# Edge keys computed behind the casts of the first weight chunk, and two row loads asked for behind chunk 4

## The chip, the core and the metric

The kernel runs on one core of a Trainium2 chip. The metric is the device time of one execution in microseconds (us). Before the change three runs gave 299.84, 299.84 and 300.05 us, so the median is 299.84.

The engines named below are TensorE (PE, with its weight loads shown as PEld), VectorE (DVE), ScalarE (ACT), GpSimd (POOL) and SyncE (SP), whose only work here is to issue transfers. Each engine runs its instructions in the order in which they were written, and waits for the others by semaphores.

## The reference, cut to what matters

One graph layer on 384 nodes with 1024 features and 16 heads of 64:

```python
h = relu(layernorm(x))
q, k, v = h @ wq.T + bq, h @ wk.T + bk, h @ wv.T + bv
q2, k2, v2 = (q @ wiq.T + biq), (k @ wik.T + bik), (v @ wiv.T + biv)   # split into 16 heads
mask = full((384, 384), -inf)
mask[src, dst] = softplus(edge_type_weights)[edge_type - 1]            # 6528 edges; of a repeated edge the last one counts
mask[i, i] = softplus(edge_type_weights)[3] where it is still -inf
out = softmax(q2 @ k2.T / 8 + mask) @ v2
return x + (out @ wo.T + bo)
```

Edges repeat, and the last of a set of equal (src, dst) pairs decides the cell. That is why the kernel compares edge keys.

## The kernel before, in words

**The dense path.** x comes in three tiles of 128 nodes. For each tile VectorE takes the statistics (`ln_bn`, `ln_mean`, L247 and L250), the mean is subtracted (`ln_sub`: ACT and POOL share tiles 0 and 1, VectorE does tile 2), TensorE transposes the tile (`ln_transpose`, L288), and the relu and the split into a high and a low part follow (`ln_hi`, L295 and L297; `ln_lo`, L302). A product in the working precision is made of three matmuls (high by high, high by low, low by high: L368 to L370). The division by the standard deviation is done later, on the products (`rrow`).

**Weights.** They are streamed in 56 chunks of 128 x 1024 (512 KB), named by a running number `w`. `load(w)` (L65) asks for one on SP's queue into one of four buffers, so that chunk w waits for the low part of chunk w - 4. `split_hi` casts a chunk to its high part (L77, on ACT), `split_lo` subtracts (L82, on VectorE or POOL). Chunk 0 is cast in two halves on VectorE (L344) and subtracted on POOL (L346). Chunks 0 and 1 go through `pieces` (L380), which orders their products by what is ready first: chunk 0 by tiles 0 and 1 (256 columns), then by tile 2, then its low part, and so on. From chunk 2 on one chunk is 24 matmuls.

**The edges.** The 6528 edges lie in 51 columns of 128; the columns are divided among three tables in DRAM of 384 x 384 cells. A key is src * 384 + dst. It is needed in two layouts: by columns on the partitions (`mask_floats`, `mask_keys` on POOL) and as rows. For the rows, `key_rows` computes 128 x 51 keys on VectorE from `er` (L180), and stores them to the DRAM tensor `krow` on SP's queue (L181). `key_load(g, s)` (L201) reads six columns of table s back, broadcast to all 128 partitions (384 KB); group 0 is loaded in the prologue, groups 1 and 2 during the projections. `mask_detect` (L213, VectorE) compares a column's keys with the row and counts later duplicates; `mask_index` (L219, L220) makes an index of it that sends overridden edges to a dump cell; `mask_scatter` (L224, POOL) writes the values to the tables, which `table_clear` (L145, SP) has cleared. The first three comparisons are written behind chunk 1's slot, one for each table. Their index shares a tile with the edge values that POOL computes (L171 to L174). Later the tables are read back and put over the mask.

**What sets the order.** The order in each engine's queue is the order of the calls in the text (`manual_schedule`); the prologue is written out by hand, and so are the slots of the projections (`slot_head`, then the products, then the edge work of the slot, `detect`). On SP's queue the prologue stands in this order: x (three tiles), `er`, chunk 0, `ed`, chunk 1, the biases, the edge type weights, the store of the keys, chunks 2 and 3, three row loads, chunk 4, then chunk 5 and the clears.

Of the kernel before, what the change touches and what calls it, by code (L numbers as in the profile page):

```python
# [14 lines left out]
N, D, NT, KT, NP = 384, 1024, 3, 8, 8  # L15
# [7 lines left out]
def gnn_kernel(ctx: ExitStack, tc: tile.TileContext, x, edges, erows, etw, wq, wk, wv, wiq, wik, wiv, wo,  # L23
# [6 lines left out]
    nc = tc.nc  # L30
# [9 lines left out]
    NTAB, RNG = 3, EC // 3  # L40
# [19 lines left out]
    def load(w):  # L60
        if w >= NCH:
            return
        n, m = chunks[w]
        raw[w] = wpool.tile([128, D], F32, tag="raw", name="raw", bufs=4)
        nc.sync.dma_start(raw[w], W[n][m])  # L65
# [112 lines left out]
    def key_rows():  # L178

        nc.vector.scalar_tensor_tensor(krt[:, :EC], er[:, :EC], float(N), er[:, EC:], op0=OP.mult, op1=OP.add)  # L180
        nc.sync.dma_start(krow.rearrange("c j -> (c j)").rearrange("(p e) -> p e", p=128), krt[:, :EC])  # L181
# [5 lines left out]
    def parts(g):  # L187
        return [(r * RNG + g * PA, min(r * RNG + (g + 1) * PA, (r + 1) * RNG)) for r in range(NTAB)]
# [3 lines left out]
    def key_load(g, s):  # L192

        if s == 0:
            t = work.tile([128, 2, NT, N], F32R, tag="pt", name="rows")
            krv[g] = t.bitcast(F32).rearrange("p a k n -> p (a k n)")
        c0, c1 = parts(g)[s]
        dst = krv[g][:, s * PA * 128:(s * PA + c1 - c0) * 128]
        for c in range(c0, c1):
            rows[c] = krv[g][:, (s * PA + c - c0) * 128:(s * PA + c - c0 + 1) * 128]  # L200
        nc.sync.dma_start(dst, krow[c0:c1, :].rearrange("c j -> (c j)").partition_broadcast(128))  # L201
# [47 lines left out]
    def ln_mean(t):  # L249
        nc.vector.bn_aggr(lnt[:, 2 * t:2 * t + 2],  # L250
                          lnt[:, 30 + 12 * t:42 + 12 * t].rearrange("p (a b) -> p a b", a=2))
        if t < 2:
            nc.scalar.mul(negm[:, t:t + 1], lnt[:, 2 * t:2 * t + 1], -1.0)
# [19 lines left out]
    def ln_sub(t, c0, c1, eng):  # L273
        src, dst = xt[t][:, c0:c1], xn[t][:, c0:c1]
        if eng is nc.scalar:
            nc.scalar.activation(dst, src, AF.Identity, bias=negm[:, t:t + 1])
        elif eng is nc.gpsimd:
            nc.gpsimd.tensor_tensor(dst, src, lnt[:, 2 * t:2 * t + 1].to_broadcast([128, c1 - c0]), OP.subtract)
        else:
            nc.vector.tensor_scalar(dst, src, lnt[:, 2 * t:2 * t + 1], None, op0=OP.subtract)  # L280

    def ln_transpose(t):
        pss = []
        for half in range(2):
            ps = bank("st"[half] if t < 2 else "ga"[half])
            for j in range(4):
                k = half * 4 + j
                nc.tensor.transpose(ps[:, j * 128:(j + 1) * 128], xn[t][:, k * 128:(k + 1) * 128], ident)  # L288
            pss.append(ps)
        return pss  # L290

    def ln_hi(t, half, ps, eng=None):
        hi = hT[:, 0, half * 4:half * 4 + 4, t * 128:(t + 1) * 128]
        if eng is None:
            nc.scalar.activation(hi, ps.rearrange("p (k n) -> p k n", k=4), AF.Relu)  # L295
        else:
            eng.tensor_scalar(hi, ps.rearrange("p (k n) -> p k n", k=4), 0.0, None, op0=OP.max)  # L297
# [28 lines left out]
    ln_bn(2, 0)  # L326
    ln_bn(2, 1)
    ln_mean(2)
    key_rows()
    load(2)  # L330
    load(3)
    for s in range(NTAB):
        key_load(0, s)
    ln_sub(2, 0, 512, nc.vector)
    ln_sub(2, 512, D, nc.vector)
    p1 = ln_transpose(1)
    warm(WARM[2])
    ln_hi(1, 0, p1[0])
# [3 lines left out]
    whl[0] = (t0[:, 0, :], t0[:, 1, :])  # L342
    for c in (slice(0, 512), slice(512, D)):
        nc.vector.tensor_copy(t0[:, 0, c], raw[0][:, c])  # L344
    for c in (slice(0, 512), slice(512, D)):
        nc.gpsimd.tensor_tensor(t0[:, 1, c], raw[0][:, c], t0[:, 0, c].bitcast(F32), OP.subtract)  # L346
    load(4)
    ln_hi(2, 0, p2[0], nc.vector)
    ln_hi(2, 1, p2[1])
    split_hi(1)  # L350
# [535 lines left out]
```

## Time and profile before

| | |
|---|---|
| median of three runs | 299.84 us |
| the profiled execution | 298.95 us |
| its span (first to last instruction) | 297.2 us |
| TensorE busy | 291.2 us, 98% of the span |
| VectorE, POOL, ACT busy | 202.4, 155.7, 153.8 us |
| share of TensorE in the chain that ended last | 96% |
| DMA, mean over the span | 185 GB/s |
| TensorE clock granted | full in every slice |

The profile page divides the span into 40 slices of 7.4 us and gives each engine's busy tenths in each. The chain that ended last is followed back from the last instruction, at each step to what released it. A timeline line has the start in us from the span's start, the time taken, the engine, the line of the kernel, the operation, what it writes and reads, how many were merged, and in brackets the idle time before it with what ended it. SPq lines are transfers that SP issues; their time is that of the issue, not of the transfer. TensorE's matmuls overlap, so that the durations of single ones add up to more than the time they take.

### The profile page before, as it was taken

The page shows a single profiled execution, that of the slowest core. Times are in us where ns is not written, and L with a number is a line of the kernel's source. Part 1 is how long each engine was busy: PE and PEld are TensorE (multiplying, and loading weights), DVE is VectorE, ACT ScalarE, POOL GpSimd, SP SyncE. Part 2 cuts the span into 40 slices and gives each one's busy share as a digit, 9 for nine tenths or more (in the row PEclk, how much of TensorE's full clock was granted, in tenths as well). Part 3 has the DMA queues.
Part 4 walks back from the last instruction along what each step waited for, and adds up shares of the span by engine and source line. Part 5 has one row for each costly group of instructions (what it writes and reads, how often), then busy time and mean ns, then how long its engine had stood idle before and what let it go on. Part 6 is the DMA issues. An engine that isn't in the chain of part 4 may idle for free.

```text
span 297.2 us, 4982 instructions
## 1 busy us (share of the span) xinstructions
PE 291.2 (98%) x1654; PEld 276.5 (93%) x1654; DVE 202.4 (68%) x495; ACT 153.8 (52%) x288; POOL 155.7 (52%) x160
## 2 busy tenths in 40 slices
PE   6999999999999999999999999999999999999995
PEld 5999999999988889999999999999999998888884
DVE  4958977766856553888865676868686766696423
ACT  3784644433422222554336677778777767865310
POOL 3774567363857785710033656373746467976210
PEclk9999999999999999999999999999999999999999
DMA  7899864645396648393369784738374656900005
GB/s 279 277 324 398 292 207 131 225 143 212 116 303 202 197 153 289 113 342 112 117 167 261 206 216 115 202 93 223 99 221 121 170 144 176 348 10 0 2 3 209
DMA packets 22377, 55.12 MB, mean 185 GB/s; under 512 B 4816, under 2 KB 8400, under 8 KB 22352
## 3 DMA queue, kind: packets, MB, share of 16 engines
q1 hardware_dynamic: 19968, 52.42, 56.0%
q0 software_dynamic: 2064, 1.80, 2.1%
q10 hardware_dynamic: 320, 0.59, 0.9%
q8 instruction: 13, 0.21, 0.3%
q14 instruction: 12, 0.10, 0.1%
HBM read 40.39 MB, written 4.97 MB: 153 GB/s over the span
## 4 chain that ended last, share of the span: by engine, by line
PE 96%; DVE 1%; DMA 1%; ACT 0%; issue 0%
PE g L370 21%; PE g L368 21%; PE g L369 21%; PE a L758 6%; PE s L721 6%; PE t L741 5%; PE g L380 3%; PE s L369 2%; PE s L370 2%; PE s L368 2%; PE t L370 2%; PE t L369 2%; PE t L368 2%; DMA g<-in_x_dram 1%; DVE lnt L247 1%; PE a L369 1%
## 5 line engine op out<-in xcount | busy, mean ns | idle before, releaser
L368 PE MATMUL g<-g,whl 128*128 128x384 f32 x304 | 103.6, 341 | 0.0
L370 PE MATMUL g<-g,whl 128*128 128x384 f32 x304 | 101.8, 335 | 0.0
L369 PE MATMUL g<-g,whl 128*128 128x384 f32 x304 | 101.5, 334 | 0.0
L224 POOL DMA_INDIRECT tab<-val,idx x51 | 56.1, 1100 | 37.5 <-issue 11.0
L77 ACT ACTIVATE whl<-raw 128x1024 fp32r<-128x1024 f32 x51 | 53.6, 1051 | 29.7 <-PE g L370 21.1
L82 DVE TENSOR_TENSOR whl<-raw,whl 128x1024 fp32r<-128x1024 f32 x41 | 52.6, 1282 | 15.6 <-ACT whl L77 12.4
L736 POOL TENSOR_TENSOR e<-e,s 128x384 f32<-128x384 f32 x48 | 39.3, 829 | 43.1 <-DVE s L735 42.4
L369 PEld LDWEIGHTS g<-g,whl 128*128 128x128 f32 x304 | 57.2, 188 | 0.0
L368 PEld LDWEIGHTS g<-g,whl 128*128 128x128 f32 x304 | 57.1, 188 | 0.0
L370 PEld LDWEIGHTS g<-g,whl 128*128 128x128 f32 x304 | 57.0, 188 | 0.0
L82 POOL TENSOR_TENSOR whl<-raw,whl 128x1024 fp32r<-128x1024 f32 x11 | 26.4, 2398 | 30.8 <-ACT whl L77 28.1
L390 ACT ACTIVATE g<-f,bc 128x384 fp32r<-128x384 f32 x24 | 14.8, 618 | 52.7 <-DVE f L389 41.2
L751 DVE TENSOR_TENSOR pt<-t,pt 128x384 fp32r<-128x384 f32 x48 | 26.4, 549 | 15.3 <-ACT pt L750 15.0
L731 ACT ACTIVATE e<-e,s 128x384 f32<-128x384 f32 x48 | 29.2, 608 | 9.3 <-DVE s L727 8.1
L750 ACT ACTIVATE pt<-t 128x384 fp32r<-128x384 f32 x48 | 23.3, 486 | 13.6 <-PE t L741 13.3
L727 DVE CUSTOM_DVE_ANT_0 e<-s,ma 128x384 f32<-128x384 f32 x48 | 26.4, 549 | 3.6 <-PE s L721 3.4
L721 PE MATMUL s<-ks,qs 128*128 128x384 f32 x96 | 24.7, 338 | 0.0
L741 PE MATMUL t<-ident,e 128*128 128x128 f32 x144 | 23.5, 271 | 0.0
L389 DVE TENSOR_TENSOR f<-g,rrow 128x384 f32<-128x384 f32 x24 | 13.3, 556 | 13.9 <-PE g L370 13.7
L741 PEld LDWEIGHTS t<-ident,e 128*128 128x128 f32 x144 | 18.7, 140 | 3.1
L758 PE MATMUL a<-pt,vhl 128*128 128x384 f32 x96 | 20.8, 351 | 0.0
L721 PEld LDWEIGHTS s<-ks,qs 128*128 128x128 f32 x96 | 17.5, 188 | 0.8
(145 smaller groups left out, 416.2 us busy)
## 6 DMA issues: line engine op xcount, KB each, us to landing
ks<-nat SPq DMA_DIRECT2D x30, 192.0 KB
raw<-in_wv_dram SPq DMA_DIRECT2D x8, 512.0 KB
raw<-in_wq_dram SPq DMA_DIRECT2D x8, 512.0 KB
raw<-in_wiv_dram SPq DMA_DIRECT2D x8, 512.0 KB
raw<-in_wk_dram SPq DMA_DIRECT2D x8, 512.0 KB
raw<-in_wiq_dram SPq DMA_DIRECT2D x8, 512.0 KB
raw<-in_wik_dram SPq DMA_DIRECT2D x8, 512.0 KB
raw<-in_wo_dram SPq DMA_DIRECT2D x8, 512.0 KB
```

Of the source, the lines that this page charges most:

```text
L77: nc.scalar.activation(dst[0], raw[w], AF.Copy)
L82: (eng or nc.vector).tensor_tensor(lo, raw[w], hi.bitcast(F32), OP.subtract)
L224: nc.gpsimd.indirect_dma_start(out=tabs[c // RNG], out_offset=bass.IndirectOffsetOnAxis(ap=idx[:, c:c + 1], axis=0), in_=val[:, c:c + 1], ...
L368: nc.tensor.matmul(ps, lhi, rhi, start=first, stop=False)
L369: nc.tensor.matmul(ps, lhi, rlo, start=False, stop=False)
L370: nc.tensor.matmul(ps, llo, rhi, start=False, stop=last)
L721: nc.tensor.matmul(ps[:, :N], qs[:, o, t * 128:(t + 1) * 128], ks[:, o, s, :], start=(s == 0), stop=(s == 1))
L727: nc.vector.tensor_tensor_reduce(e, st_ps.pop(i)[:, :N], ma[:, t, :], -0.125, 3.0e38, OP.add, OP.min, s[:, 0:1])
L731: nc.scalar.activation(es[i], es[i], AF.Exp, bias=s[:, 0:1], scale=-1.0, accum_out=s[:, 1:2])
L736: nc.gpsimd.tensor_tensor(es[i], es[i], s[:, 2:3].to_broadcast([128, N]), OP.mult)
L741: nc.tensor.transpose(ps[:, k * 128:(k + 1) * 128], es[i][:, k * 128:(k + 1) * 128], ident)
L758: nc.tensor.matmul(ps[:, :N], vhl[:, k, p, 2 * o:2 * o + 2, :], pts[h][:, s, k, :], start=(k == 0 and s == 0), stop=(k == 2 and s == 1))
```

## The change

`key_rows()` (one VectorE instruction and the store that SP issues) goes from just behind the statistics of tile 2 to just behind the two casts of chunk 0 on VectorE. The subtraction of tile 2's mean and the loads of chunks 2 and 3 so come ahead of it. Of the three row loads of group 0, the one for table 0 follows the store, and those for tables 1 and 2 are asked for behind chunk 4. Nothing is added and nothing removed.

```diff
@@ -326,13 +326,10 @@
     ln_bn(2, 0)
     ln_bn(2, 1)
     ln_mean(2)
-    key_rows()
+    ln_sub(2, 0, 512, nc.vector)
+    ln_sub(2, 512, D, nc.vector)
     load(2)
     load(3)
-    for s in range(NTAB):
-        key_load(0, s)
-    ln_sub(2, 0, 512, nc.vector)
-    ln_sub(2, 512, D, nc.vector)
     p1 = ln_transpose(1)
     warm(WARM[2])
     ln_hi(1, 0, p1[0])
@@ -342,9 +339,13 @@
     whl[0] = (t0[:, 0, :], t0[:, 1, :])
     for c in (slice(0, 512), slice(512, D)):
         nc.vector.tensor_copy(t0[:, 0, c], raw[0][:, c])
+    key_rows()
+    key_load(0, 0)
     for c in (slice(0, 512), slice(512, D)):
         nc.gpsimd.tensor_tensor(t0[:, 1, c], raw[0][:, c], t0[:, 0, c].bitcast(F32), OP.subtract)
     load(4)
+    key_load(0, 1)
+    key_load(0, 2)
     ln_hi(2, 0, p2[0], nc.vector)
     ln_hi(2, 1, p2[1])
     split_hi(1)
```

## The prediction

> **What bounds the kernel now.** I read the page first (engine shares, the 40 slices, the chain that ended last), then the chain in order of time for the first 20 us, then the timeline of that stretch engine by engine, with SP's queue, and last the busy times by stretches of 1 us with the DMA rate.
>
> ```profile
> PE 291.2 (98%) x1654; PEld 276.5 (93%) x1654; DVE 202.4 (68%) x495; ACT 153.8 (52%) x288; POOL 155.7 (52%) x160
> PE   6999999999999999999999999999999999999995
> PE 96%; DVE 1%; DMA 1%; ACT 0%; issue 0%
> ```
>
> TensorE is the bound: full in every slice but the first and the last, and 96% of the chain. So a change counts only if it moves TensorE's first real matmul, or opens a gap later. The chain of the first 20 us shows the first:
>
> ```profile
> 8.23 0.66 PE s L288 x4
> 8.89 0.45 PE t L288 x4
> 9.34 0.63 PE g L288 x4
> 9.97 0.44 PE a L288 x4
> 10.41 8.16 PE g L380 x52
> ```
>
> From 8.23 on TensorE follows itself: transposes of tiles 1 and 2, then the products of w0 and w1, then everything else. The timeline shows what feeds them, and the other ends of the change:
>
> ```profile
> 8.46 0.21 DVE L250 BATCH_NORM_AGGREGATE lnt<-lnt 128x2 f32<-128x12 f32 x1
> 8.59 0.16 DVE L180 SCALAR_TENSOR_TENSOR kr<-er 128x51 f32<-128x51 int32 x1
> 8.71 0.88 DVE L280 TENSOR_SCALAR g<-g,lnt 128x512 f32<-128x512 f32 x2
> 8.78 0.33 SPq L181 DMA_DIRECT2D krow<-kr  x1
> 9.15 0.91 SPq L65 DMA_DIRECT2D raw<-in_wv_dram  x2
> 9.31 0.42 PEld L288 LDWEIGHTS g<-ident,g 128*128 128x128 f32 x4 [0.22 <-issue]
> 9.51 0.76 DVE L344 CAST whl<-raw 128x512 fp32r<-128x512 f32 x2
> 10.01 2.66 POOL L346 TENSOR_TENSOR whl<-raw,whl 128x512 fp32r<-128x512 f32 x2 [1.70 <-DVE whl L344]
> 10.69 1.29 SPq L201 DMA_DIRECT2D rows<-krow  x3
> 12.70 2.70 SPq L65 DMA_DIRECT2D raw<-in_wv_dram  x2
> 13.85 1.06 ACT L77 ACTIVATE whl<-raw 128x1024 fp32r<-128x1024 f32 x1 [1.49 <-DMA raw<-in_wv_dram]
> 23.34 1.06 ACT L77 ACTIVATE whl<-raw 128x1024 fp32r<-128x1024 f32 x1 [0.56 <-DMA raw<-in_wv_dram]
> 23.80 0.17 DVE L219 SCALAR_TENSOR_TENSOR ed<-cnt,key 128x3 f32<-128x3 f32 x1 [0.83 <-POOL val L174]
> ```
>
> The reader is to see: VectorE goes from the statistics of tile 2 (L250) through the key (L180) to the subtraction (L280) that tile 2's transposes at 9.31 wait for; SP issues nothing between 5.42 (4.96 + 0.46, the issue before) and 8.78, and its waits put 3.1 us there on the key of L180; two casts on ACT wait for weights (chunk 2 until 13.85, chunk 4 until 23.34).
>
> **The change part by part.**
>
> *The key leaves the place ahead of L280.* L280 starts 0.12 after L180 (8.71 - 8.59), so the most to be had is 0.12 us. But L280 reads the mean that L250 ends at 8.67 (8.46 + 0.21). In pairs where the second reads the first's result, the second starts 0.04 after the first's end: L219 23.80 + 0.17 to L220 at 24.01; L166 17.97 + 0.16 to L167 at 18.17. 8.67 + 0.04 = 8.71: where L280 stands today. L180, which does not read the mean, sits in that bubble (it starts 0.08 before L250 ends). Bounds: gain 0.00 to 0.12. I take 0.00, by the two dependent pairs, which are the same situation.
>
> The Trainium skill (VectorE: DVE Perf Modes, "The DRAIN you can't avoid" and the rules for authors) says that chained operations pay for emptying the pipe and that their count is what to lower; by that, one operation fewer ahead of L280 would be worth all of its 0.16. The trace agrees only in part, since L180 overlaps L250.
>
> *The key comes in behind the casts of w0* (now 9.51 to 10.27). It adds 0.12 (its start-to-start) ahead of ln_hi(2,0), L297, now 10.18 + 0.69 = 10.87, then 10.99. Behind L297 are the six low parts of h (L302), the root's follow-up and softplus_a, all 0.12 later until VectorE's idle time after 16.84. Who waits: TensorE's second pass of w0 (tile 2) comes after eight 256-column products, which the groups by shape give 1.2 us of busy time, 293 ns each; the last overlaps the next one's start, so the pass starts no sooner than 10.16 + 1.2 - 0.29 = 11.07. 10.99 leaves 0.08: cost 0, bound 0.1. The low parts end at 13.77 + 0.68 = 14.45, then 14.57; the last half is first used 16 matmuls of 0.173 ahead of 18.57, at 15.8: hidden by 1.2 us. POOL's L346 starts on the first cast, which lies ahead of the key and stays at 9.51: 0.
>
> *Chunks 2 and 3 no longer stand behind the key on SP.* Their two issues (0.91 together) go from 9.15 to just behind 5.42, at the latest behind the landing of x's last tile (VectorE starts on it at 7.14). The DMA rate by stretches is 378 GB/s in 6 to 8, 419 in 8 to 9, 116 in 9 to 10, 66 in 10 to 11: the queue runs dry there today, and these 2 x 512 KB fill the hole. From 10 on, 1.05 MB at 378 GB/s take 2.8 us: they land at about 12.8, chunk 2 at about 11.4. ACT's cast of chunk 2 can then start where ACT falls idle, at 13.85 - 1.49 = 12.36. What is late next: the softplus table (1.28) is loaded by 14.7, and L160 waits for softplus_a, 15.55 + 0.15 + 0.12 = 15.82, against 16.22 now. So 0.4 us earlier for ACT, POOL's values (L174) and the cast and low part of chunk 3. TensorE meets chunk 3 at 23.61, with the low part now ready at 20.44 + 1.22 = 21.66: the gain is only more slack, 0 on the sum.
>
> *The key's store.* L180 at about 10.18 releases the store on SP 0.19 later (8.59 to 8.78), 10.4; it queues behind chunks 2 and 3 and lands at about 13.3 instead of 10.69 (I allow half a us behind them). Then on SP: rows of table 0 (0.43), chunk 4 (0.33), rows 1 and 2 (0.86), from 13.3 to 14.9. Chunk 4 is issued at 13.8 instead of 12.70; chunk 5 waits for POOL until 15.06 anyway; the clears of the tables follow as now. So the queue behind the waiting SP loses nothing but chunk 4's 1.1 us, and chunk 4 gains the two row loads that it no longer stands behind.
>
> *When do the third table's rows land?* VectorE reads them at 22.59. Behind the issue at 13.3 lie at most 1.9 us (store issued to its release, 8.78 to 10.69), so data flow from 15.2 at the latest; 3 x 384 KB + 512 KB = 1.70 MB. Rates of rows: 194 and 226 GB/s in 16 to 18, where they have the queue, 324 and 347 in 18 to 20, mixed with weights. At 194 they end at 24.0, at 226 at 22.7, at 324 at 20.4. I take 22.5, between the last two, since a third of the bytes are weights.
>
> The Trainium skill (DMA: Bandwidth & Descriptors, "Specifications") has packets of 512 B and more at line rate; the rows' 3 KB packets would then end by 20. In the trace 16 to 18 contradicts it; the sum is the same by both.
>
> At 22.5 the third comparison ends at about 23.0, still before 23.80, where L219 waits for POOL's values (perhaps 23.4 with the 0.4 above). What it would cost with that cover gone: from L219 VectorE is busy through to the low part of chunk 5, 29.36 + 1.22 = 30.58. Chunk 2 starts on TensorE at 19.45 and chunk 3 at 23.61, so a chunk is 4.16 and chunk 5 starts at 31.93; weights load 0.18 ahead. Slack 1.17. L219 may slip to 24.97, so the rows may land until 24.5 before TensorE waits. Cost 0, with nothing to gain where TensorE has no gap; upper bound +0.5 (landing at 25, 1.0 beyond the slowest rate).
>
> **The sum.** 0.00 (L280; bound -0.12) + 0.00 (second pass; bound +0.10) + 0 (all DMA; bound +0.5). Against the profiled execution: 298.95 us (span 297.2 and 1.75 around it) stays 298.95, which stands 0.89 below the median of 299.84. Predicted median: 299.8.
>
> **The rivals.**
> 1. *The key's 0.12 does come off the start:* L280 at 8.59, tile 2's transposes and the casts 0.12 earlier, TensorE with them; ACT's last cast ahead of w0 (L295, 9.52 + 0.61 = 10.13) does not stop it, being needed only from the fifth matmul on. 299.84 - 0.12 = 299.72. For it: TensorE waits 0.22 before 9.31. Against: the dependent pairs.
> 2. *Slower, by the late third table:* its rows land after 24.5, VectorE stands in line behind the comparison, the low part of chunk 5 comes late. Landing at 26 costs 1.5: 301.3; just past the point, 300.0. For it: three row loads begin 2.6 us later than now, and a rows stretch at 194 GB/s ends at 24.0, 0.5 short of the point. Against: the slack, and chunks 2 and 3 already out of the queue.
> 3. *Really faster:* ACT's two waits for weights (1.49 and 0.56) were paid for by TensorE; then up to 2.0 less, 297.8. Against it: PE shows no idle time between 8.23 and the end, and every chunk's low part is ready 1.2 us or more ahead. Only small gaps below what the views print could hide it, so a fraction at best: 299.2.
>
> **How the numbers follow.** Main case (nothing on TensorE's path, 299.7 to 299.95) 0.70; rival 1 0.10; rival 2 0.12; rival 3 0.05; 0.03 is left for a shift of clock or code that no view announces, taken as within 0.2%. 0.2%, 0.6 us, is about what a measurement of this kernel can tell from no change. Main case, rival 1 and the remainder lie within it: 0.83, and rival 2 just past its point too, so of its 0.12 0.02 go there: same 0.85, slower 0.10, faster 0.05. The range goes from 299.3 (a fraction of rival 3) to 300.5 (the rows half a us past their point, 299.84 + 0.5, rounded up).
>
> **What would show it.** Right: L280 starts again 0.25 after L250, w0's first L380 again at 10.1 to 10.2; L180 behind the casts; SP's two chunk issues between 5.4 and 7.5; the store landed at 13 to 13.7; ACT's wait of 1.49 gone; L219 again held by POOL's values; PE without a gap. Wrong: L280 at 8.6 (rival 1); VectorE idle before L213 with the rows as releaser, L219 after 25, TensorE idle near 32 (rival 2); chunks starting on TensorE at less than 4.16 apart (rival 3).

## The result and the profile after

The changed kernel takes 300.72 us (median of 20 runs, 299.86 to 301.07) against 299.86 for the kernel before (20 runs beside it, 299.18 to 300.33). The ratio is 1.0024, 95% interval 1.0016 to 1.0032: slower by 0.5 to 1.0 us. The forecast was no change (299.8, range 299.3 to 300.5), so it was wrong: the loss is clear of noise, and the time lies above the range. The profiled execution of the change took 300.95 us with a span of 299.2.

From the page of the changed kernel: busy time of each engine, TensorE in 40 slices, and the chain that ended last.

```profile
PE 291.1 (97%) x1654; PEld 276.4 (92%) x1654; DVE 203.0 (68%) x495; ACT 153.8 (51%) x288; POOL 155.0 (52%) x160
PE   6799999999999999999999999999999999999995
PE 94%; DMA 2%; DVE 2%; SPq 0%; issue 0%
```

TensorE does the same work (291.1 us against 291.2) in a span 2.0 longer; the loss stands at the start, where the second slice is no longer full (7 instead of 9), and VectorE and the transfers have 2% of the chain each instead of 1%. The chain of the changed kernel in order of time shows the place (start, duration, what):

```profile
9.72 0.88 DVE g L280 x2
10.60 0.67 DVE whl L341 x2
11.27 1.22 DVE kr L180
12.50 0.61 DVE g L297
...
13.15 6.89 PE g L381 x41
```

The key, L180, is a link of 1.22 us between the casts of chunk 0 and the relu of tile 2 (L297), and TensorE's products wait for that relu. The timeline of the changed kernel, engine by engine:

```profile
8.15 1.29 DVE L247 BATCH_NORM_STATS2 lnt<-g 128x6 f32<-128x512 f32 x2 [1.10 <-DMA g<-in_x_dram]
9.47 0.21 DVE L250 BATCH_NORM_AGGREGATE lnt<-lnt 128x2 f32<-128x12 f32 x1
9.72 0.88 DVE L280 TENSOR_SCALAR g<-g,lnt 128x512 f32<-128x512 f32 x2
11.02 2.65 POOL L345 TENSOR_TENSOR whl<-raw,whl 128x512 fp32r<-128x512 f32 x2 [2.84 <-DVE whl L341]
11.15 1.01 PEld L381 LDWEIGHTS g<-g,whl 128*128 128x128 f32 x8
11.19 1.31 DVE L180 SCALAR_TENSOR_TENSOR kr<-er 128x51 f32<-128x51 int32 x1
13.15 1.11 PE L381 MATMUL g<-g,whl 128*128 128x128 f32 x8 [0.78 <-DVE g L297]
21.27 0.19 PEld L369 LDWEIGHTS g<-g,whl 128*128 128x128 f32 x1
25.30 0.17 DVE L219 SCALAR_TENSOR_TENSOR ed<-cnt,key 128x3 f32<-128x3 f32 x1 [0.83 <-POOL val L174]
```

The same instruction on 128 x 51 that took 0.16 us takes 1.31 here. It comes 0.17 after POOL's subtraction L345 has started, and TensorE waits 0.78 before its second pass of chunk 0.

Two distances sort the 2.0 us. From TensorE's first weight load of chunk 0 to that of chunk 2 (L368 before, L369 after) pass 9.13 us before (10.14 to 19.27) and 10.12 after (11.15 to 21.27): 0.99 lost there. From chunk 2 to the end of the span it is 277.9 in both (297.2 - 19.27 and 299.2 - 21.27): nothing that happens later matters. The other 1.01 us lies ahead of the first product, 10.14 against 11.15, where VectorE starts on x's third tile at 8.15, after a wait of 1.10 for it, instead of 7.14 without a wait. Whether that belongs to the change had to be found out.

### The profile page after: what moved, and what is told of

The parts are those of the page before. It is cut to its first block, busy times and chain, and to the rows that moved or that the text cites. A ratio compares the mean times of both kernels' runs of the same rounds, so it can differ in the third digit from the quotient of the medians.

```text
span 299.2 us, 4982 instructions
## 1 busy us (share of the span) xinstructions
PE 291.1 (97%) x1654; PEld 276.4 (92%) x1654; DVE 203.0 (68%) x495; ACT 153.8 (51%) x288; POOL 155.0 (52%) x160
## 4 chain that ended last, share of the span: by engine, by line
PE 94%; DMA 2%; DVE 2%; SPq 0%; issue 0%
PE g L369 21%; PE g L371 21%; PE g L370 21%; PE a L759 6%; PE s L722 6%; PE t L742 5%; PE g L381 3%; DMA g<-in_x_dram 2%; PE s L370 2%; PE s L371 2%; PE s L369 2%; PE t L371 2%; PE t L370 2%; PE t L369 2%; PE a L371 1%; PE a L370 1%
## 5 line engine op out<-in xcount | busy, mean ns | idle before, releaser
L369 PE MATMUL g<-g,whl 128*128 128x384 f32 x304 | 103.6, 341 | 0.0
L82 DVE TENSOR_TENSOR whl<-raw,whl 128x1024 fp32r<-128x1024 f32 x41 | 52.4, 1277 | 15.3 <-ACT whl L77 15.3
L369 PEld LDWEIGHTS g<-g,whl 128*128 128x128 f32 x304 | 57.1, 188 | 0.0
L82 POOL TENSOR_TENSOR whl<-raw,whl 128x1024 fp32r<-128x1024 f32 x11 | 26.4, 2399 | 30.4 <-ACT whl L77 27.7
L751 ACT ACTIVATE pt<-t 128x384 fp32r<-128x384 f32 x48 | 23.3, 486 | 13.6 <-PE t L742 13.3
L390 DVE TENSOR_TENSOR f<-g,rrow 128x384 f32<-128x384 f32 x24 | 13.3, 555 | 14.2 <-PE g L371 14.2
```

Of the source, the lines that this page charges most:

```text
L82: (eng or nc.vector).tensor_tensor(lo, raw[w], hi.bitcast(F32), OP.subtract)
L369: nc.tensor.matmul(ps, lhi, rhi, start=first, stop=False)
```

## The experiments

Theory A: the key, behind the casts, stands still beside POOL's subtraction of chunk 0 and holds up the relu of tile 2. Theory B: the early loads of chunks 2 and 3 make x's third tile land late. Theory C: the late rows of the tables. What the kernels gave (d is the time from the first weight load of chunk 0 to that of chunk 2, in the traced execution; the ratio is against the kernel before, timed on the same chip):

| run | key or added instruction, us | d, us | ratio, 95% interval |
|---|---|---|---|
| kernel before | 0.16 | 9.13 | |
| the change | 1.31 | 10.12 | 1.0024 (1.0016 to 1.0032) |
| key at its old place, SP as changed | 0.16 | 9.11 | 0.9999 (0.9989 to 1.0009) |
| key ahead of the casts | 0.20 | 9.21 | 0.9999 (0.9988 to 1.0011) |
| before, with a second key behind the casts | 1.31 | 10.12 | 1.0026 (1.0014 to 1.0039) |
| key through PSUM | 0.20 and 0.21 | 9.29 | 0.9995 (0.9983 to 1.0006) |
| POOL's subtraction in one piece | 0.21 | 9.90 | 1.0015 (1.0006 to 1.0025) |
| in four pieces | 0.21; again 0.75 | 9.07; again 9.56 | 1.0018 (1.0008 to 1.0028) |
| before, with a one-input copy behind the casts | 1.28 | 10.02 | 1.0017 (1.0006 to 1.0028) |
| 768 and 256 columns | 0.21 | 9.19 | 1.0010 (0.9996 to 1.0024) |
| before, 23 warm-up transposes | 0.16 | 9.11 | 0.9991 (0.9980 to 1.0002) |

### The two halves of the change apart

The key back at its old place, every transfer as in the change:

```diff
     ln_mean(2)
+    nc.vector.scalar_tensor_tensor(krt[:, :EC], er[:, :EC], float(N), er[:, EC:], op0=OP.mult, op1=OP.add)
     ln_sub(2, 0, 512, nc.vector)
...
     def key_rows():
-        nc.vector.scalar_tensor_tensor(krt[:, :EC], er[:, :EC], float(N), er[:, EC:], op0=OP.mult, op1=OP.add)
         nc.sync.dma_start(krow...
```

> The key's VectorE instruction goes back between the statistics and the subtraction of tile 2; SP's order stays that of the change (chunks 2 and 3 ahead of the store, rows 1 and 2 behind chunk 4). Theory A (the key behind the casts stands still beside POOL's subtraction of chunk 0 and holds up the relu of tile 2, so TensorE's second pass of chunk 0): the key takes 0.16 us again, no gap of TensorE between the first and the second pass, time that of the kernel before within 0.15 us. Theory B (the early loads of chunks 2 and 3 make x's third tile land 1.0 us later, 8.1 instead of 7.1, and with it everything): time 0.7 to 1.0 us above the kernel before. Theory C (the late rows): also 0.7 to 1.0 above, with VectorE waiting for rows.

And the other way round: the kernel before, every transfer in its place, with one more instruction of the key's form:

```diff
         nc.vector.tensor_copy(t0[:, 0, c], raw[0][:, c])
+    scrap = ert[:, 2 * EC:3 * EC]
+    nc.vector.scalar_tensor_tensor(scrap, er[:, :EC], float(N), er[:, EC:], op0=OP.mult, op1=OP.add)
     for c in (slice(0, 512), slice(512, D)):
```

> The kernel before with one more instruction of the key's form (two SBUF inputs, 128 x 51) behind the casts of chunk 0, written to unused columns; no transfer is moved. Theory A: the added instruction takes 1.2 to 1.4 us instead of 0.16, the relu of tile 2 starts 1.2 later, TensorE waits 0.8 to 1.1 before the second pass, time 0.7 to 1.0 us above the kernel before. Theories B and C: 0.16 us for the added instruction and no change of the time beyond 0.15.

The timelines, first of the key at its old place:

```profile
7.82 1.29 DVE L246 BATCH_NORM_STATS2 lnt<-g 128x6 f32<-128x512 f32 x2 [0.85 <-DMA g<-in_x_dram]
9.27 0.16 DVE L328 SCALAR_TENSOR_TENSOR kr<-er 128x51 f32<-128x51 int32 x1
10.82 8.08 PEld L381 LDWEIGHTS g<-g,whl 128*128 128x128 f32 x52
19.93 0.19 PEld L369 LDWEIGHTS g<-g,whl 128*128 128x128 f32 x1
```

then of the kernel before with the second key (L346 is the added one, L348 POOL's subtraction):

```profile
8.12 1.29 DVE L247 BATCH_NORM_STATS2 lnt<-g 128x6 f32<-128x512 f32 x2 [1.00 <-DMA g<-in_x_dram]
9.56 0.16 DVE L180 SCALAR_TENSOR_TENSOR kr<-er 128x51 f32<-128x51 int32 x1
10.98 2.64 POOL L348 TENSOR_TENSOR whl<-raw,whl 128x512 fp32r<-128x512 f32 x2 [2.74 <-DVE whl L344]
11.15 1.31 DVE L346 SCALAR_TENSOR_TENSOR er<-er 128x51 f32<-128x51 int32 x1
11.11 1.02 PEld L382 LDWEIGHTS g<-g,whl 128*128 128x128 f32 x8
13.11 7.09 PEld L382 LDWEIGHTS g<-g,whl 128*128 128x128 f32 x44 [0.98 <-DVE g L297]
21.23 0.19 PEld L370 LDWEIGHTS g<-g,whl 128*128 128x128 f32 x1
```

All of SP's part gives 0.9999; one instruction behind the casts, alone, gives 1.0026 and the d of the change to the hundredth. The same operation takes 0.16 at 9.56 and 1.31 at 11.15 in one execution, so neither its form nor its size is the cost, but the place. B and C fall. x's third tile was late in the second of these (8.12) with SP's queue exactly as before.

### The key ahead of the casts

```diff
     ln_sub(2, 512, D, nc.vector)
+    nc.vector.scalar_tensor_tensor(krt[:, :EC], er[:, :EC], float(N), er[:, EC:], op0=OP.mult, op1=OP.add)
     load(2)
```

(and gone from `key_rows`, which keeps the store.)

> The change, but the key's instruction stands between the subtraction of tile 2 and the casts of chunk 0, where POOL is idle. Theory A: the key takes 0.16 us; the casts start 0.12 later; no gap of TensorE between the passes; 0 to 0.15 us above the kernel before. Theories B and C: 0.7 to 1.0 us above.

It took 0.20 us, and 0.9999 is the time of before. Moving the key out of the wait for the mean was worth nothing, and what it cost ahead of the casts is too little to be seen (d is 0.08 longer in the one trace; the interval reaches about 0.35 us either way).

### Which instructions wait

SBUF and PSUM are the two on-chip memories that the kernel uses: most tiles lie in SBUF, the results of TensorE in PSUM. The key of the change, made by two instructions of which neither reads two SBUF tensors:

```diff
-        nc.vector.scalar_tensor_tensor(krt[:, :EC], er[:, :EC], float(N), er[:, EC:], op0=OP.mult, op1=OP.add)
+        kps = bank("g")
+        nc.vector.tensor_scalar(kps[:, :EC], er[:, :EC], float(N), None, op0=OP.mult)
+        nc.vector.scalar_tensor_tensor(krt[:, :EC], kps[:, :EC], 1.0, er[:, EC:], op0=OP.mult, op1=OP.add)
```

> The change, but the key is made behind the casts by two instructions with one SBUF input each: the product of src goes to PSUM, then PSUM times 1 plus dst. If it is two SBUF inputs that make the instruction wait for POOL (theory A, narrow form): both take 0.1 to 0.25 us, TensorE's wait before the second pass is at most 0.2, time 0 to 0.25 us above the kernel before. If any VectorE instruction on SBUF at that place waits (theory A, wide form): 1.2 us again, 0.7 to 1.0 above. Theories B and C: 0.7 to 1.0 above.

A copy with one input, added to the kernel before:

```diff
         nc.vector.tensor_copy(t0[:, 0, c], raw[0][:, c])
+    nc.vector.tensor_copy(ert[:, 2 * EC:3 * EC], krt[:, :EC])
     for c in (slice(0, 512), slice(512, D)):
```

> The kernel before with one float copy of 128 x 51 from SBUF to SBUF (one input) added behind the casts of chunk 0. If only two SBUF inputs make VectorE wait for POOL: the copy takes 0.1 to 0.2 us, no wait of TensorE, the time of the kernel before within 0.15 us. If one input of a fast SBUF copy is enough: 1.2 to 1.4 us, TensorE waits 0.8 to 1.1, time 0.7 to 1.0 us above.

The timeline of the key through PSUM:

```profile
10.28 2.66 POOL L347 TENSOR_TENSOR whl<-raw,whl 128x512 fp32r<-128x512 f32 x2 [2.00 <-DVE whl L343]
10.45 0.20 DVE L181 TENSOR_SCALAR g<-er 128x51 f32<-128x51 int32 x1
10.69 0.21 DVE L182 SCALAR_TENSOR_TENSOR kr<-g,er 128x51 f32<-128x51 f32 x1
10.41 8.26 PEld L383 LDWEIGHTS g<-g,whl 128*128 128x128 f32 x52
```

and of the one-input copy (L345):

```profile
11.04 2.64 POOL L347 TENSOR_TENSOR whl<-raw,whl 128x512 fp32r<-128x512 f32 x2 [2.97 <-DVE whl L344]
11.21 1.28 DVE L345 COPY er<-kr 128x51 f32<-128x51 f32 x1
13.14 7.11 PEld L381 LDWEIGHTS g<-g,whl 128*128 128x128 f32 x44 [0.88 <-DVE g L297]
```

Two instructions with one SBUF input and one side in PSUM pass POOL's subtraction at 0.20 and 0.21 us, at the same place, 0.17 behind its start. The copy from SBUF to SBUF, with one input, stands still like the key: the narrower reading, that only two inputs make it wait, fell. (The timed loss of that kernel, 0.5 us by the ratio with 0.2 to 0.8, is smaller than the 0.7 to 1.0 expected.) The Trainium skill (SBUF - State Buffer, "Who interferes with whom") states the rule that fits both: VectorE and GpSimd share one pair of SBUF ports, held for a whole instruction; VectorE needs it for two SBUF inputs (against a GpSimd instruction that reads SBUF) and for copies in a two-port mode, and whoever comes second is blocked. These traces agree, with 1.31 and 1.28 us for those two forms and 0.2 for the others; that the copy ran in a two-port mode is not seen in any view.

### How long it waits, and who comes first

POOL's subtraction in one instruction of 1024 columns:

```diff
-    for c in (slice(0, 512), slice(512, D)):
+    for c in (slice(0, D),):
         nc.gpsimd.tensor_tensor(t0[:, 1, c], raw[0][:, c], t0[:, 0, c].bitcast(F32), OP.subtract)
```

> The change, with POOL's subtraction of chunk 0 as one instruction of 1024 columns in place of two of 512. If the key waits for the end of the POOL instruction that is running when it comes: the key takes 2.3 to 2.6 us instead of 1.31, TensorE's wait before the second pass grows from 1.0 to 2.0 to 2.2, time 1.7 to 2.1 us above the kernel before. If the 1.31 us is a fixed cost of that instruction at that place: no difference from the change, 0.7 to 0.9 above the kernel before.

This did not test what it was meant to. The one instruction reads both casts, so it started behind the key, not ahead of it:

```profile
11.25 0.21 DVE L180 SCALAR_TENSOR_TENSOR kr<-er 128x51 f32<-128x51 int32 x1
11.42 2.39 POOL L345 TENSOR_TENSOR whl<-raw,whl 128x1024 fp32r<-128x1024 f32 x1 [3.19 <-DVE whl L341]
13.86 6.22 PEld L381 LDWEIGHTS g<-g,whl 128*128 128x128 f32 x36 [0.72 <-POOL whl L345]
```

With POOL not yet running the key takes 0.21, and TensorE pays elsewhere: it waits 0.72 for the low part of chunk 0. The time, 0.45 us above the kernel before by the ratio, is neither of the two expected. Here only POOL's instruction was made another, its start moved behind the key's, and the key's wait was gone. Four pieces of 256 columns:

```diff
-    for c in (slice(0, 512), slice(512, D)):
+    for c in (slice(0, 256), slice(256, 512), slice(512, 768), slice(768, D)):
         nc.gpsimd.tensor_tensor(t0[:, 1, c], raw[0][:, c], t0[:, 0, c].bitcast(F32), OP.subtract)
```

> The change, with POOL's subtraction of chunk 0 in four instructions of 256 columns. If the key waits for the running POOL instruction only: the key takes 0.5 to 0.8 us, TensorE's wait is 0.2 to 0.4, time 0 to 0.4 us above the kernel before. If it waits for POOL to fall idle: 2.5 us and more, 1.7 to 2.1 above. If the cost is fixed: 1.31 again, 0.7 to 0.9 above.

> The change with POOL's subtraction in four pieces of 256 once more, for its trace. In the first one the key slipped in ahead of POOL and took 0.21 us, while the time was still above the kernel before. If which of the two comes first changes from execution to execution: here 0.5 to 0.8 us for the key is possible, and 9.3 to 9.6 us from the first product of chunk 0 to that of chunk 2; if the key always slips in: 0.2 and 9.1.

The two traces of this one kernel, the first:

```profile
9.90 3.06 POOL L345 TENSOR_TENSOR whl<-raw,whl 128x256 fp32r<-128x256 f32 x4 [1.61 <-DVE whl L341]
10.07 0.21 DVE L180 SCALAR_TENSOR_TENSOR kr<-er 128x51 f32<-128x51 int32 x1
```

and the second:

```profile
10.79 2.94 POOL L345 TENSOR_TENSOR whl<-raw,whl 128x256 fp32r<-128x256 f32 x4 [2.37 <-DVE whl L341]
10.96 0.75 DVE L180 SCALAR_TENSOR_TENSOR kr<-er 128x51 f32<-128x51 int32 x1
12.36 7.09 PEld L381 LDWEIGHTS g<-g,whl 128*128 128x128 f32 x44 [0.43 <-DVE g L297]
```

In both the key is listed 0.17 behind POOL's start. In the first it slipped in and POOL's first piece paid (966 ns, against 856 in the second and 737 in the median); in the second it waited for that piece, 0.75. So the wait ends with POOL's running instruction and goes by its length: 0.75 with 256 columns, where the piece ends at 11.65 (10.79 + 0.86) and the key at 11.71; 1.31 with 512, where the piece ends at 12.43 (11.02 + 1.41) and the key at 12.50. The listed starts do not say who goes first. POOL's piece may not have got going at its listed start: VectorE's second cast is still running there (until 11.28 in the change), and POOL's first piece is 0.12 longer than the next of its size (1407 against 1282 ns); that the cast holds it is not shown. Nor is it shown why the four pieces are 0.2% slower in the timed runs; executions in which the key loses would be a part of it.

The last of the kind, casts and subtraction as 768 and 256 columns:

```diff
-    for c in (slice(0, 512), slice(512, D)):
+    for c in (slice(0, 768), slice(768, D)):
         nc.vector.tensor_copy(t0[:, 0, c], raw[0][:, c])
...
-    for c in (slice(0, 512), slice(512, D)):
+    for c in (slice(0, 768), slice(768, D)):
         nc.gpsimd.tensor_tensor(t0[:, 1, c], raw[0][:, c], t0[:, 0, c].bitcast(F32), OP.subtract)
```

> The change, with the casts of chunk 0 and POOL's subtraction divided into 768 and 256 columns instead of 512 and 512, so that POOL's first instruction, which starts before the key, is longer by half. If the key waits for the end of the running POOL instruction: it takes 1.8 to 2.1 us instead of 1.31, and from TensorE's first product of chunk 0 to its first of chunk 2 pass 10.6 to 10.9 us instead of 10.1; time 1.2 to 1.7 us above the kernel before. If the 1.31 is fixed: 10.1 again, 0.7 to 1.0 above.

A miss: the second cast is shorter, the key came only 0.04 behind POOL's listed start (11.12 against 11.08) and won, 0.21 us. That a longer running instruction makes the wait longer than 1.31 was thus not shown; only the shorter one was.

### The start of the profile, and a longer warm-up

The kernel before and the changed kernel once more, unaltered:

> The kernel before once more, for its trace. Where the landing of x's third tile (7.1 us in the first trace of before, 8.1 in that of the change) differs from execution to execution of the same text, it lies between 7.1 and 8.2 here too, and the span follows it. If the early loads of chunks 2 and 3 were its cause, 7.1 again.

> The changed kernel once more, for its trace. The key takes 1.2 to 1.4 us again and from TensorE's first product of chunk 0 to its first of chunk 2 pass 10.0 to 10.2 us, whenever x's third tile lands (7.0 to 8.2).

The kernel before, second trace:

```profile
6.61 1.12 PE L288 MATMUL s<-ident,g 128*128 128x128 f32 x4 [0.65 <-ACT g L276]
7.89 1.29 DVE L247 BATCH_NORM_STATS2 lnt<-g 128x6 f32<-128x512 f32 x2 [0.66 <-DMA g<-in_x_dram]
11.23 8.04 PEld L380 LDWEIGHTS g<-g,whl 128*128 128x128 f32 x52
20.29 0.19 PEld L368 LDWEIGHTS g<-g,whl 128*128 128x128 f32 x1
```

The changed kernel, second trace:

```profile
10.99 2.64 POOL L345 TENSOR_TENSOR whl<-raw,whl 128x512 fp32r<-128x512 f32 x2 [2.85 <-DVE whl L341]
11.16 1.31 DVE L180 SCALAR_TENSOR_TENSOR kr<-er 128x51 f32<-128x51 int32 x1
11.12 1.02 PEld L381 LDWEIGHTS g<-g,whl 128*128 128x128 f32 x8
21.24 0.19 PEld L369 LDWEIGHTS g<-g,whl 128*128 128x128 f32 x1
```

The text of before starts its first product at 11.23 here, and at 10.14 in the first trace: the 1.01 us ahead of the first product is not the change. d is 9.06 and 10.12, as in the first traces. The first profile of before, 298.95 us, was simply an early one for a median of 299.86.

In this second trace of before TensorE's transposes at 6.6 take 1.7 times as long as in the first (four in 1.12 against 0.66), at a granted clock that is listed as 1.00 in both. This suggested three more warm-up transposes, `WARM = (23, 3, 0)`:

> The kernel before with 23 transposes of the identity at the start instead of 20, so that TensorE is busy until just before its first real transposes at 6.6 even where each takes 213 ns. In three traces of the second set those real transposes still took 213 ns until 10, in all others 109. If the gap between the 20 and 6.6 lets the clock stay low in part of the executions, this ends it: median 0.1 to 0.5 us below the kernel before. If the start is set by the landing of x's third tile alone: the same time within 0.15 us.

299.44 against 299.66, ratio 0.9991, interval 0.9980 to 1.0002: no verdict. One trace of it has a first product at 10.01 with the transposes fast; that is one execution, and it is left open.

## Why the prediction was wrong, point by point

**The step that failed** is "The key comes in behind the casts of w0 ... It adds 0.12 (its start-to-start)". The 0.12 was read from a row in which POOL is idle (it has no line between 8.31 and 10.01). At the new place the term measures 1.31, so the relu of tile 2 is 1.2 later, the slack of 0.08 that was to be left of the second pass is gone, and d grows by 0.99. The slack itself was sized about right: 0.20 without the key (11.07 - 10.87). Counted from the first weight load the relu comes 1.23 later in the change (0.04 behind it before, 1.27 after) and costs 0.99; in the second trace of the four pieces it comes 0.67 later and costs 0.43. So 0.24 was hidden both times, and the term that was mis-sized is the key's own time. The bound set there, 0.1, came from the same row and so was no bound. The same paragraph looked at POOL's L346 only for whether the key delays POOL, not for whether POOL delays the key.

The profile of before held rows that say so. The timeline of before, a few us further on, where small instructions of one engine stand beside the other's subtraction of a chunk (L82, two SBUF inputs):

```profile
12.63 2.40 POOL L82 TENSOR_TENSOR whl<-raw,whl 128x1024 fp32r<-128x1024 f32 x1
...
14.64 0.41 DVE L262 TENSOR_TENSOR lnt<-lnt 128x3 f32<-128x3 f32 x1
...
15.63 1.21 DVE L82 TENSOR_TENSOR whl<-raw,whl 128x1024 fp32r<-128x1024 f32 x1
15.87 1.12 POOL L153 TENSOR_TENSOR key<-ed 128x51 f32<-128x51 f32 x1
...
19.49 0.29 POOL L174 TENSOR_TENSOR val<-val,ed 128x51 f32<-128x51 f32 x1
...
20.44 1.22 DVE L82 TENSOR_TENSOR whl<-raw,whl 128x1024 fp32r<-128x1024 f32 x1 [2.10 <-ACT whl L77]
20.45 1.37 POOL L174 TENSOR_TENSOR val<-val,ed 128x51 f32<-128x51 f32 x1
```

L174 takes 0.29 alone and 1.37 when it comes 0.01 behind VectorE's L82, until 0.16 after L82's end; L153, of the same size, takes 1.12 beside L82. In the changed kernel L153 falls ahead of L82 and takes 0.29 (16.84 against 17.60). Those are POOL's instructions held by VectorE. The direction of the key is in L262, which also reads two SBUF tensors, of 3 columns: it takes 0.41 and ends 0.02 after POOL's L82 (15.05 against 15.03). In the second trace of before it takes 0.22, and again ends with POOL's L82 (15.79 against 15.78); in the trace of the one-input copy, where that L82 had ended, it takes 0.16. By such rows the bound would have been the length of POOL's instruction beside the key, 1.3 us (half of L346's 2.66).

**The key leaves the place ahead of L280: gain 0.00.** Right. L280 starts 0.25 after L250 with the key between them (8.46 to 8.71) and without it (9.47 to 9.72). The rival of 0.12 gained falls, and so does the value of 0.16 that the rule on emptying the pipe would have given.

**Chunks 2 and 3 early on SP.** Right in kind: issued from 5.71, ACT's wait of 1.49 is gone (chunk 2 is cast at 13.48 without a wait). But L160 waits 1.87 for softplus_a and runs at 17.71 in place of 16.22: what is late next is VectorE, by the key's 1.2 and this execution's late start. The whole of SP's part is worth nothing, as the sum had it: 0.9999 with the key at its old place.

**The store and the rows.** Off in time, harmless in effect. The store was issued at 12.52, not 10.4, since it waits for the key; rows of table 0 followed at 14.95, not 13.3. The third table's rows held up nobody: the comparisons start at 23.54 in a row, and L219 at 25.30 waits 0.83 for POOL's values, as before. The slower rival named the right sign and the wrong mechanism; the one that came was in no case of mine, and the 0.10 for slower stood for something else.

**TensorE is the bound and hides the rest.** Right: 277.9 to 278.0 us from chunk 2 to the end in both traces of before and both of the change. Wrong was to take the slack of the second pass as enough without asking who else holds VectorE at that moment.

What stays open: the traces of the change lose 0.99 us, the timed runs 0.5 to 1.0 (0.72 by the ratio, 0.86 by the medians). The added instructions show the same: 0.99 and 0.89 in their traces, 0.78 and 0.51 by the ratio. Executions in which the key wins against POOL would explain it; with two pieces of 512 none of the four traces (two of the change, two of added instructions) shows one.

## What to carry to other kernels

Price a moved VectorE instruction at its new place, with what POOL runs there: one that reads two SBUF tensors, or copies from SBUF to SBUF, can stand still until POOL's running instruction ends, however small it is (here beside a subtraction of two SBUF tensors). Look in the trace for one short instruction with two durations (0.29 and 1.37 here); what stands beside the long one is the price. Where such an instruction has to stand there, give it a PSUM side (0.20 here), or put it where POOL waits.

## What was not expected of the hardware

- A one-input copy of 128 x 51 from SBUF to SBUF took 1.28 us beside POOL's subtraction, as long as the two-input key.
- With the same distance of 0.17 us between listed starts the key once went ahead of POOL (0.21 us) and once waited (0.75): the order of two listed starts does not tell who goes first.
- The prologue differs by 1.1 us between executions of one text (first product at 10.14 and 11.23), through the landing of x's third tile (7.14 and 7.89) and the pace of TensorE's first transposes (0.66 and 1.12 us for four). A difference of two profiles of this kernel below that size says nothing unless the stretch is cut at the first product.
